# Attention scores with heads of eight: two fp32 products replaced by three bfloat16 passes over split operands

## The chip, the cores and the metric

The kernel runs on one core of one Trainium2 chip. The metric is the device time of one execution in microseconds (us). Before the change three executions took 1519.76 us in the median (1519.46 to 1520.83).

A core has five engines with their own instruction streams, each in order: TensorE (PE, matrix products; its weight loads are listed as PEld), VectorE (DVE), ScalarE (ACT), GpSimd (POOL) and SyncE (SP), which here issues most transfers (DMA). They wait for one another through semaphores. TensorE takes a stationary operand (lhsT) and streams a moving one (rhs); it writes to the eight banks of PSUM, from which DVE and ACT read. An operand that takes only 32 of the 128 partitions uses one of four row tiles of the array.

## The reference

A decoder of four layers, batch 4, sequence 256, model width 128, 16 heads of size 8, and a context of 512 rows for cross attention. Each layer is self attention, cross attention and a feed-forward part. What matters here are the attentions of layers 0 and 3, which all have this form:

```python
x = x + _L0_attn_ref(_layernorm(x), W_qkv, b_qkv, W_proj, b_proj)
x = x + _L0_xattn_ref(_layernorm(x), ctx, mask, q_w, q_b, kv_w, kv_b, proj_w, proj_b)
...
def _L0_xattn_ref(x, context, context_mask, ...):
    q = (x @ q_w + q_b).reshape(b, n, h, d)                  # h = 16, d = 8
    kv = (context @ kv_w + kv_b).reshape(b, s, 2, h, d)
    attn = jnp.einsum('bnhd,bshd->bhns', q, k) * scale
    attn = jnp.where(context_mask[:, None, None, :], -jnp.inf, attn)
    attn = jax.nn.softmax(attn, axis=-1)
    out = jnp.einsum('bhns,bshd->bnhd', attn, v).reshape(b, n, c)
    return out @ proj_w + proj_b
```

Layer 0's self attention has no mask, its cross attention a mask over keys. Layer 3's self attention makes q, k and v through a latent of width 32 and has a causal mask; its cross attention has a full mask over queries and keys. Layer 1 (with a clipped softmax), layer 2 and the feed-forward parts are not touched by the change, apart from when layer 0's expert weights are loaded.

## The kernel before

**Units.** `woven` (L394) runs a layer's attentions as a list of eight units: units 0 to 3 are the self attentions of the four batch rows (256 keys), units 4 to 7 their cross attentions (512 keys). Layers 0 and 3 use it so; layer 1 uses it for its own self attention.

**Operands.** A unit's prelude normalises x (statistics on DVE, the rest on POOL), transposes it, and makes queries (`queries`, L412: a product L343, an ACT pass L423 that scales and adds the bias, then four POOL products L426 that write `qm`, four copies of q, in each of which only one head of every group of four is not zero) and keys (`keys`, L428: a product and an ACT pass L434 into `kc`). A row tile of 32 partitions holds four heads; with the masked copy number g as one operand and all 32 partitions of `kc` as the other, a product gives the scores of one of the four.

**Rows.** `rows_of` (L454) computes scores with queries on partitions, in fp32 (L471), 512 columns in a bank of PSUM. DVE takes the maximum over keys: L478 without a mask, L482 with one (layer 3). In layer 0's cross attention the key mask is added by a bfloat16 product ahead of it (L465). `parts` (L494) splits the maxima into three bfloat16 parts on DVE, and `parts_T` (L505) transposes them on TensorE (L509) into `mT`.

**Columns.** `columns_of` (L514) computes the scores again, transposed (keys on partitions): two small bfloat16 products subtract the maxima (L530, from `mT`), one fp32 product adds the scores (L536), in layer 3 after a mask product (L523). ACT takes the exponential from PSUM (L553, or L555 with the key mask as a bias in layer 0's cross attention). `weighted` (L566; products L572) multiplies by the values and a column of ones, `divided_by_sums` (L580) transposes and divides, `added` (L604) projects and adds to x.

An fp32 product stands in the trace as two PE instructions.

**Order.** The order of TensorE's instructions is written by position. In window n, the columns of unit n run beside the rows of unit n+1 (all but the first LEAD = 2 half groups) and the first LEAD half groups of unit n+2. `beat` (L627) pairs a half group of rows (two of the four row tiles) with a half group of columns (the other two), so that all four row tiles are in use. A self window has 8 beats, the window of unit 3 has 12, cross windows 16; the last has 8 beats of columns alone. Into these the prelude of unit n+2 is spread by `front` (L677) over the first 0.95 of the window less the lead; unit 1's prelude goes into the first 0.8 of the start, where unit 0's rows run alone. Rows that have their operands not yet hold TensorE, and with it everything that is behind them. Scores use seven banks of PSUM ("s1"), a beat takes four.

**Loads around it.** `layer_0` (L2124) loads the key mask and then, in eight transfers of 1 MB, the experts' first weights `e0h` (L2129); they are used by `ffn0` (L1266), which begins by loading the second weights `e0d` (4 MB) and computes a shared expert and 32 experts. SP issues these, and the transfers of the normalised rows to DRAM (`sent`).

Of the kernel before, what the change touches and what calls it, by code (L numbers as in the profile page):

```python
# [31 lines left out]
P = 128  # L33
B, S, D, H = 4, 256, 128, 16
NT = B * S // P
SK = 512
# [33 lines left out]
def _constants():  # L70

    p = np.arange(P)
    l = np.arange(1, S + 1, dtype=np.float32)
    angle = (np.pi / 2 * l / S).astype(np.float32)
    trig = np.stack([np.sin(angle), np.cos(angle)], -1)
    trig = trig.reshape(2, P, 2).transpose(1, 0, 2).reshape(P, 4)
    ident = np.eye(P)

    tril = np.where(p[:, None] <= p[None, :], 10.0, NEG)
    m72 = np.repeat((p[:, None] // 16) == np.arange(8)[None, :], 9, axis=1)  # L80
    m4 = (p[:, None] // 32) == np.arange(4)[None, :]
    iota = np.tile(np.arange(P), (P, 1))
    gm = (p[:, None] // 8 % 4) == np.arange(4)[None, :]
    gs = -1.0 * ((p[:, None] % 4 == np.arange(4)[None, :]) & (p[:, None] % 32 < 12))
    after = p[:, None] < p[None, :]
    upto = np.concatenate([after[:, :32], p[:, None] <= p[None, :32]], 1)
    parts = (ident, tril, m72, m4, iota, trig, gm, gs, p[:, None], after, upto)
    return _cat(*[a.astype(np.float32) for a in parts])
# [3 lines left out]
    _C_IDENT, _C_TRIL, _C_M72, _C_M4, _C_IOTA, _C_TRIG, _C_GM, _C_GS, _C_PART, _C_AFTER, _C_UPTO,  # L92
    _C_END,
) = np.cumsum([0, 128, 128, 72, 4, 128, 4, 4, 4, 1, 128, 64]).tolist()


def _layout(i):
# [16 lines left out]

    w, bq = f["L0_attn_W_qkv"], f["L0_attn_b_qkv"]
    a["w0a"] = _cat(w, f["L0_attn_W_proj"], _col(bq[:128]), _col(bq[128:256]))
    w, bk = f["L0_xattn_kv_w"], f["L0_xattn_kv_b"]
    a["w0x"] = _cat(
        f["L0_xattn_q_w"], w, f["L0_xattn_proj_w"], _col(f["L0_xattn_q_b"]), _col(bk[:128])
# [12 lines left out]
        f[k + "Wq"].T, f[k + "Wk"].T, f[k + "Wv"].T, f[k + "Wo"].T,  # L132
        _col(f[k + "bq"]), _col(f[k + "bk"]),
# [8 lines left out]
    up[:32, :128] = f["L3_attn_Wq_up"].T  # L142
    up[32:64, :128] = f["L3_attn_Wk_up"].T
# [40 lines left out]
def decoder(ctx: ExitStack, tc: tile.TileContext, dr, out):  # L184
# [57 lines left out]
    partition = cst[:, _C_PART:_C_AFTER]  # L242
# [109 lines left out]
    def key_mask(pool, name, keep):  # L352

        rows_ = pool.tile([P, B * SK // 4], I32, tag="mrow", name="mrow", bufs=1)
        nc.sync.dma_start(rows_, dr[name].to_broadcast([P, B * SK // 4]))
        cols = pool.tile([P, B * NKT // 4], I32, tag="mcol", name="mcol", bufs=1)
        nc.sync.dma_start(cols, dr[name + "T"])
        out = []
        for t, dtype in ((rows_, BF16), (cols, F32)):
            t = t.bitcast(U8)  # L360
            m = pool.tile(list(t.shape), dtype, tag=f"n{t.shape[1]}", name=f"n{t.shape[1]}", bufs=1)
            if keep:
                V.tensor_scalar(m, t, 0.0, NEG, ALU.is_equal, ALU.mult)
            else:
                V.tensor_scalar(m, t, NEG, None, ALU.mult)
            out.append(m)
        return out
# [9 lines left out]
    class Unit:  # L377
# [7 lines left out]
        def __init__(u, b, nk, weights, prelude, context, q_bias=None, k_bias=None, v_bias=None,  # L385
                     rows_mask=None, row_mask=None, cols_mask=None, key_bias=None, clip=False):
            u.b, u.nk, u.weights, u.prelude, u.context = b, nk, weights, prelude, context
            u.q_bias, u.k_bias, u.v_bias = q_bias, k_bias, v_bias
            u.rows_mask, u.row_mask, u.cols_mask = rows_mask, row_mask, cols_mask
            u.key_bias, u.clip, u.nkt = key_bias, clip, nk // P  # L390
            u.mx, u.pr, u.po = None, {}, {}

            u.beside, u.after, u.within = [], [], 2.6

    def woven(pool, units, n_keys):
# [4 lines left out]
        for i in range(2):  # L400
            t = pool.tile([P, n_keys // P, H, 32], F32, tag=f"v{i}", name=f"v{i}", bufs=1)
            V.memset(t, 0.0)
            V.memset(t[:, :, :, HD : HD + 1], 1.0)
            vbuf.append(t)
            t = pool.tile([P, 2, 4, 32], BF16, tag=f"mp{i}", name=f"mp{i}", bufs=1)
            V.memset(t, 0.0)
            mbuf.append(t)

# [3 lines left out]
        def queries(u):  # L412
# [11 lines left out]
            u.qm = pool.tile([P, 4, S], F32, tag="qm", name="qm", bufs=3)  # L424
            for g in range(4):
                G.tensor_scalar(u.qm[:, g, :], q, gmask[:, g : g + 1], None, ALU.mult)  # L426

        def keys(u):  # L428
            acc = product(u.weights[1], u.key_source, "s1")
            u.kc = pool.tile([P, u.nk], F32, tag="kc", name="kc", bufs=3)  # L430
            if u.k_bias is None:
                A.copy(u.kc, acc)
            else:
                A.activation(u.kc, acc, AF.Identity, bias=u.k_bias)  # L434

# [18 lines left out]
        def rows_of(u, qt, g, half):  # L454
# [5 lines left out]
            head, tail, reads = [], [], []  # L460
            for j, r in row_tiles(half):
# [25 lines left out]
                steps = [call(score, i) for i in range(per)]  # L487
                if u.row_mask is not None:
                    steps = [mask] + steps
                head.append(steps[0])  # L490
                tail += steps[1:]
                reads.append(read)
            return [], head, tail, reads

        def parts(u):
# [3 lines left out]
            V.tensor_copy(mp[:, :, :, 0:4], u.mx)  # L499
            r1 = small.tile([P, 2, 4, 4], F32, tag="r1", name="r1")  # L500
            V.tensor_tensor(r1, u.mx, mp[:, :, :, 0:4], ALU.subtract)
            V.tensor_copy(mp[:, :, :, 4:8], r1)
            V.tensor_tensor(mp[:, :, :, 8:12], r1, mp[:, :, :, 4:8], ALU.subtract)

        def parts_T(u):  # L505
            mp = mbuf[u.n % 2]
            tp = psum[0].tile([P, 1024], BF16, tag="s1", name="s1", bufs=BANKS["s1"])
            for qt in range(2):
# [3 lines left out]
            u.mT = pool.tile([P, S], BF16, tag="mT", name="mT")  # L512
            evacuate(u.mT, tp[:, :S])

        def columns_of(u, gp, kt, half):

            first = kt * P if u.clip else 0
            masks, heads, reads = [], [[], [], []], []
            for j, r in row_tiles(half):
# [21 lines left out]
                def read(j=j, sc=sc):  # L541
# [10 lines left out]
                    elif u.key_bias is None:  # L552
# [3 lines left out]

                if u.cols_mask is not None:
                    masks.append(mask)
                if not u.clip:
                    heads[0].append(call(less, 0))  # L560
                    heads[1].append(call(less, 1))
                heads[2].append(score)
                reads.append(read)
            return masks, heads[0] + heads[1] + heads[2], [], reads
# [62 lines left out]
        def beat(*steps):  # L627

            made = [f(half) for f, half in steps]
            for k in range(3):  # L630
                for m in made:
                    for f in m[k]:
                        f()
            for pair in zip(*[m[3] for m in made]):
# [43 lines left out]
        def front(n):  # L678
# [3 lines left out]
            if n + 2 < len(units):  # L682
                out += spread(prelude(units[n + 2]), 0.0, 0.95 - lead)
# [29 lines left out]
        for n, u in enumerate(units):  # L713
            u.n = n
# [4 lines left out]
        if len(units) > 1:  # L719
            first += spread(prelude(units[1]), 0.0, 0.8)  # L720
# [545 lines left out]
    def ffn0(r, wh):  # L1266
        with ExitStack() as st:
            pool = expert_pools(st, "ffn0")
            wd = load("e0d", pool=pool)
# [854 lines left out]
    def layer_0(wh, router):  # L2124
        with ExitStack() as st:
            st.enter_context(psum_pool("ps0"))
            pool = attn_pool(st, "l0")
            neg0, neg0T = key_mask(pool, "mbk0", False)
            for i in range(0, 32, 4):  # L2129
                cols = slice(i * 512, (i + 4) * 512)  # L2130
                nc.sync.dma_start(wh[:, cols], dr["e0h"][:, cols])
# [6 lines left out]
            for u in units[:B]:  # L2138
                u.beside = [call(context_means, u.b, 0), call(context_means, u.b, 2)]
                u.beside += [call(context_scales, u.b)]  # L2140
            for u in units[B:]:
                u.beside = [call(normalise_context, u.b, i) for i in range(0, NKT, 2)]
                u.after, u.within = router.steps(pool, u.b, "s1"), 1.0
            woven(pool, units, SK)
# [17 lines left out]
    def layer_3():  # L2162
        with ExitStack() as st:
# [13 lines left out]
            woven(pool, units, SK)  # L2177
# [47 lines left out]
```

## Time and profile before

Times are of one profiled execution unless said otherwise.

| what | us |
|---|---|
| median of three executions | 1519.76 |
| the profiled execution | 1519.6 |
| its span in the trace | 1517.5 |
| layer 0, both attentions | 0 to 276 |
| layer 0, experts | 276 to 348 |
| layer 3, from the end of layer 2 | 1174 to 1517.5 |
| DVE busy in layer 0's attentions | 177.4 |
| DVE busy in layer 3 | 192.7 |
| mean granted TensorE clock | 0.927 of full speed |

The rest, from 348 to 1174 us, is layers 1 and 2. A line of the profile's groups reads: source line, engine, operation, output <- inputs with the shapes (partitions x elements; for a product partitions of contraction * partitions of output, then the moving operand), x count, then busy time in us and mean ns of one, then the idle time of the engine just before them and what ended most of it. A line of a window reads: stretch, its length, busy us and instructions of PE, PEld, DVE, ACT, POOL, granted clock, share of the DMA engines in use, GB/s. The chain of waits is the chain of work that ended last, followed back from the last instruction to what released each.

### The profile page before, as it was taken

How to read it: one execution, taken by the hardware profiler on the slowest of the kernel's cores; microseconds unless marked ns; L12 is line 12 of the kernel's file. 1: busy time of each engine (PE TensorE's matmuls, PEld its weight loads, DVE VectorE, ACT ScalarE, POOL GpSimd, SP SyncE). 2: the span in 40 equal slices, each digit the busy share in tenths (PEclk: the TensorE clock that was granted, in tenths of full speed). 3: DMA queues.
4: the chain of work that ended last, by engine and by line, in shares of the span. 5: the costliest groups of instructions: out<-in, count | busy, mean ns of one | idle time of the engine just before them, and what ended most of it. 6: DMA issues, size and time to landing. Idle time of an engine off the chain costs nothing.

```text
span 1517.5 us, 27226 instructions
## 1 busy us (share of the span) xinstructions
PE 1336.0 (88%) x10232; PEld 696.3 (46%) x10232; DVE 814.4 (54%) x2688; ACT 736.5 (49%) x1468; POOL 307.0 (20%) x433
## 2 busy tenths in 40 slices
PE   5999998796787997889999999999595699999994
PEld 3544333353353664545555565555364344433332
DVE  6687773585664447454544454460334556756633
ACT  0555666285542333267667757666021044345553
POOL 6322111354133215000000000000332513111000
PEclk7999999896996999989999999999698589999996
DMA  8000000320222124320111000000311000000000
GB/s 329 4 2 1 2 5 8 125 58 11 118 105 91 37 71 168 119 83 15 57 46 43 1 5 1 1 5 1 134 45 51 28 1 2 2 1 2 5 5 7
DMA packets 35315, 67.97 MB, mean 45 GB/s; under 512 B 5349, under 2 KB 19087, under 8 KB 33263
## 3 DMA queue, kind: packets, MB, share of 16 engines
q1 hardware_dynamic: 30770, 49.88, 9.2%
q0 software_dynamic: 3264, 6.69, 2.0%
q10 hardware_dynamic: 1152, 9.67, 1.6%
q8 instruction: 82, 1.34, 0.4%
q14 instruction: 47, 0.39, 0.1%
HBM read 49.55 MB, written 16.68 MB: 44 GB/s over the span
## 4 chain that ended last, share of the span: by engine, by line
PE 70%; DVE 10%; ACT 7%; POOL 6%; issue 4%; DMA 3%; SPq 0%; ACTq 0%; POOLq 0%; DVEq 0%
PE o L572 7%; PE s L536 7%; PE s L471 6%; PE o L1894 6%; PE g L1159 6%; PE s L1874 4%; PE f L1820 4%; PE y L1183 3%; PE s L523 3%; PE f L1806 2%; PE s L530 2%; DVE mx L478 2%; PE t L1168 2%; PE s L343 2%; PE s L1867 1%
## 5 line engine op out<-in xcount | busy, mean ns | idle before, releaser
L471 PE MATMUL s<-kc,qm 32*128 32x256 f32 (+1 forms) x1024 | 222.8, 565 | 13.6 <-DVE mx L482 6.5
L553 ACT ACTIVATE pr<-s 128x512 f32<-128x512 f32 x256 | 138.0, 596 | 187.0 <-PE s L536 184.2
L536 PE MATMUL s<-qm,kc 32*128 32x512 f32 (+1 forms) x896 | 208.8, 607 | 0.0
L293 POOL TENSOR_SCALAR ve<-mv 128x2 f32<-128x2 f32 x44 | 11.7, 266 | 789.3 <-DVE mv L288 784.3
L1831 ACT ACTIVATE ss<-ss,ntop 128x768 f32<-128x768 f32 x128 | 118.6, 928 | 90.0 <-DVE ntop L1829 89.8
L478 DVE TENSOR_REDUCE mx<-s 128x1 f32<-128x512 f32 (+1 forms) x192 | 122.6, 685 | 59.1 <-PE s L536 47.0
L572 PE MATMUL o<-pr,v 128*32 128x256 f32 (+1 forms) x1792 | 145.1, 391 | 8.9 <-ACT os L578 4.2
L471 PEld LDWEIGHTS s<-kc,qm 32*128 32x128 f32 x1024 | 91.2, 207 | 71.7 <-DVE mx L482 18.9
L1825 DVE CUSTOM_DVE_ANT_0 ss<-f,n 128x512 f32<-128x512 f32 x128 | 83.5, 689 | 68.4 <-PE f L1820 68.4
L482 DVE CUSTOM_DVE_ANT_0 junk<-s,nmif 128x512 bf16<-128x512 f32 x128 | 83.1, 688 | 47.5 <-PE s L471 47.3
L1894 PE MATMUL o<-pr,v 128*64 128x256 f32 x768 | 107.1, 392 | 1.3 <-ACT pr L1881 1.2
L555 ACT ACTIVATE pr<-s,n 128x512 f32<-128x512 f32 x128 | 80.2, 690 | 51.3 <-PE s L536 32.0
L1874 PE MATMUL s<-qT,kT 64*128 64x256 f32 x768 | 101.1, 379 | 0.0
L1881 ACT ACTIVATE pr<-s,n 128x512 f32<-128x512 f32 x128 | 80.3, 678 | 25.6 <-PE s L1874 25.3
L572 PEld LDWEIGHTS o<-pr,v 128*32 128x32 f32 x1792 | 40.1, 109 | 112.5 <-issue 83.4
L426 POOL TENSOR_SCALAR qm<-q,consts 128x256 f32<-128x256 f32 x64 | 58.5, 930 | 153.3 <-ACT q L423 123.0
L530 PE MATMUL s<-mT,selg 12*128 12x256 bf16 x768 | 80.8, 276 | 2.9 <-DVE mx L478 0.8
L1137 POOL DMA_INDIRECT xb<-sent,token x62 | 60.5, 977 | 104.1 <-PE t L1144 58.5
L1820 PE MATMUL f<-kT,qT 64*128 64x512 f32 x256 | 77.2, 625 | 2.3 <-ACT kT L273 1.1
L1813 DVE CUSTOM_DVE_ANT_0 ss<-f,nought 128x256 f32<-128x256 f32 x128 | 46.7, 421 | 55.4 <-PE f L1806 53.9
L1894 PEld LDWEIGHTS o<-pr,v 128*64 128x64 f32 x768 | 47.7, 136 | 57.2 <-issue 21.7
L536 PEld LDWEIGHTS s<-qm,kc 32*128 32x128 f32 x896 | 67.2, 194 | 6.3 <-issue 3.3
(455 smaller groups left out, 2424.9 us busy)
## 6 DMA issues: line engine op xcount, KB each, us to landing
e0h<-in_e0h SPq DMA_DIRECT2D x8, 1024.0 KB, 10.7
kd<-ahead SPq DMA_DIRECT2D x20, 256.0 KB, 2.4
vd<-ahead SPq DMA_DIRECT2D x20, 256.0 KB, 2.6
kT<-kd SPq DMA_DIRECT2D x20, 256.0 KB, 4.3
v<-vd SPq DMA_DIRECT2D x5, 1024.0 KB, 5.3
e0d<-in_e0d SPq DMA_DIRECT2D x1, 4096.0 KB
e1h<-in_e1h ACTq DMA_DIRECT2D x1, 4096.0 KB
done<-ys SPq DMA_DIRECT2D x14, 256.0 KB, 2.3
```

Of the source, the lines that this page charges most:

```text
L471: T.matmul(sc[:, i, :], lhsT=u.qm[r, g + i, qt * P : (qt + 1) * P], rhs=u.kc[r, :], start=u.row_mask is None, stop=True,)
L478: V.tensor_reduce(u.mx[:, qt, j, g : g + per], sc, AX.X, ALU.max)
L530: T.matmul(sc[:, i, :], lhsT=selg[r, gp + i, :], rhs=u.mT[r, :], start=u.cols_mask is None and i == 0, stop=False,)
L536: T.matmul(sc, lhsT=u.kc[r, kt * P : (kt + 1) * P], rhs=u.qm[r, gp : gp + 2, first:], start=u.clip, stop=True,)
L553: A.activation(dst, sc, AF.Exp)
L572: T.matmul(u.po[gp][32 * j : 32 * j + 32, i, first:], lhsT=u.v[:, kt, 4 * j + gp + i, :], rhs=u.pr[gp, kt, j][:, i, first:], start=kt + i ...
L1159: T.matmul(p[r], lhsT=xbT[b][:, r], rhs=w(512 * i), start=biases is None, stop=True,)
L1820: T.matmul(sc[h], lhsT=qT[u, c][hrow[h], qt * P : (qt + 1) * P], rhs=kT[u, c][hrow[h], :SK], start=True, stop=True,)
L1825: V.tensor_tensor_reduce(ss[qt][h][:, :SK], sc[h], neg1[:, b * SK : (b + 1) * SK], 1.0, -3e38, ALU.add, ALU.max, accum_out=mx[:, qt, h, 1:2],)
L1831: A.activation(ss[qt][h], ss[qt][h], AF.Exp, bias=ntop[:, qt, h, c : c + 1], accum_out=total[:, qt, h, c : c + 1],)
L1874: T.matmul(sc[h][:, i, :], lhsT=kT[u, c][hrow[h], kt * P : (kt + 1) * P], rhs=qT[u, c][hrow[h], :], start=False, stop=i == 1,)
L1894: T.matmul(po[u, g][hrow[h], i, :], lhsT=v[u][:, kt, n * hd : (n + 1) * hd], rhs=pr[u, g, kt, h][:, i, :], start=kt + i == 0, stop=kt + i ...
```

## The change

In layers 0 and 3, for all units but the first of each layer:

- q and k are each written as a sum of three bfloat16 parts (`in_parts`, on POOL: copy, subtract, copy, subtract).
- The parts go to DRAM (one transfer for q, one for k) and are read back so that, in a row tile of 32 partitions, partition 4·d + i holds element d of a head in slot i: the q operand `q3[c]` repeats part c in the slots 0 to 2, the k operand `kk` holds the parts 0 to 2 in them; the four heads of the row tile lie side by side in the free dimension. One product of 32 partitions thus makes three of the nine products of parts, and three of them, one for each `q3[c]`, make all nine. That takes nine reads for q and three for k.
- Slot 3 carries constants (`rest`, loaded once) on one side and, on the other, the key mask (layer 0's cross attention, one read more) or the parts of the maxima. These are brought by eight transposes and one DVE addition (`qmax`), so that the subtraction of the maximum and the key mask need no products of their own. The exponential has no bias any more.
- The weights' columns are permuted in the inputs (`byd`), so that a head's eight elements lie where the reads want them.
- `beat` deals out the products round by round, rows and columns in turn.
- The prelude of a split unit is spread over the first 0.4 of a self window or 0.55 of a cross window, unit 1's over the first 0.3 of the start.
- Three sets of parts are kept. In layer 0 they lie in the second half of the tile of `e0h`, and so does the key mask: the first half of `e0h` is loaded beside unit 0, the second half in `ffn0`, between the two halves of `e0d`. In layer 3 they lie in the normalised context and `w2kv`, which are no longer used.

```diff
+        def in_parts(src, tag, m):
+            n = src.shape[1]
+            t = pool.tile([P, 3, m], BF16, tag=tag, name=tag)[:, :, :n]
+            G.tensor_copy(t[:, 0], src)
+            G.tensor_tensor(src, src, t[:, 0], ALU.subtract)
+            G.tensor_copy(t[:, 1], src)
+            G.tensor_tensor(t[:, 2], src, t[:, 1], ALU.subtract)
+            return t
...
         def queries(u):
...
-            u.qm = pool.tile([P, 4, S], F32, tag="qm", name="qm", bufs=3)
+            if u.split:
+                u.q3 = qbuf[u.n % 3]
+                to = qd[u.n % 3]
+                nc.sync.dma_start(to.rearrange("c f n -> f c n"), in_parts(q, "qp", S))
+                for c in range(3):
+                    for i in range(3):
+                        nc.sync.dma_start(
+                            u.q3[c][i::4], to[c].rearrange("(x g) n -> x g n", g=4)
+                        )
+                return
+            u.qm = pool.tile([P, 4, S], F32, tag="qm", name="qm", bufs=1 if split else 3)
...
         def keys(u):
...
+            if u.split:
+                u.kk = kbuf[u.n % 3]
+                to = kd[u.n % 3][:, :, : u.nk]
+                nc.sync.dma_start(to.rearrange("c f n -> f c n"), in_parts(u.kc, "kp", SK))
+                for c in range(3):
+                    nc.sync.dma_start(
+                        u.kk[c::4, :, : u.nk], to[c].rearrange("(x g) n -> x g n", g=4)
+                    )
+                if u.row_mask is not None:
+                    nc.sync.dma_start(
+                        u.kk[15::32, :, : u.nk],
+                        u.row_mask[0:4].unsqueeze(1).to_broadcast([4, 4, u.nk]),
+                    )
...
         def rows_of(u, qt, g, half):
...
+                def part(n, r=r, sc=sc):
+                    i, c = n // 3, n % 3
+                    T.matmul(
+                        sc[:, i, :], lhsT=u.q3[c][r, g + i, qt * P : (qt + 1) * P],
+                        rhs=u.kk[r, g + i, : u.nk], start=n == 0, stop=n == 3 * per - 1,
+                    )
+
+                if u.split:
+                    for n in range(3 * per):
+                        rounds.setdefault(2 * n // per, []).append(call(part, n))
...
         def parts_T(u):
...
+            if u.split:
+                for qt in range(2):
+                    for g in range(4):
+                        T.transpose(
+                            tp[:, g * S + qt * P : g * S + (qt + 1) * P],
+                            mp[:, qt, g].rearrange("p j c -> p (j c)"), identb,
+                        )
+
+                u.qmax = pool.tile([P, 4, S], BF16, tag="qmax", name="qmax")
+                V.tensor_tensor(
+                    u.qmax, tp.rearrange("p (g n) -> p g n", g=4), u.q3[2], ALU.add
+                )
+                return
...
         def columns_of(u, gp, kt, half):
...
+                def part(n, r=r, sc=sc):
+                    c, i = n // 2, n % 2
+                    T.matmul(
+                        sc[:, i, :], lhsT=u.kk[r, gp + i, kt * P : (kt + 1) * P],
+                        rhs=(u.q3[0], u.q3[1], u.qmax)[c][r, gp + i, :],
+                        start=u.cols_mask is None and n == 0, stop=n == 5,
+                    )
...
+                if u.split:
+                    for n in range(6):
+                        rounds.setdefault(n, []).append(call(part, n))
...
         def front(n):
...
-                out += spread(prelude(units[n + 2]), 0.0, 0.95 - lead)
+                u = units[n + 2]
+                end = 0.95 - lead if not u.split else 0.4 if units[n].nk < SK else 0.55
+                out += spread(prelude(u), 0.0, end)
...
-            u.n = n
+            u.n, u.split = n, split and n > 0
...
-            first += spread(prelude(units[1]), 0.0, 0.8)
+            first += spread(prelude(units[1]), 0.0, 0.3 if split else 0.8)
...
     def ffn0(r, wh):
...
-            wd = load("e0d", pool=pool)
+            wd = pool.tile([P, 32 * 256], F32, tag="e0d", name="e0d", bufs=1)
+            for i in range(0, 32, 16):
+                cols = slice(i * 256, (i + 16) * 256)
+                nc.sync.dma_start(wd[:, cols], dr["e0d"][:, cols])
+                if i == 0:
+                    cols = slice(16 * 512, 32 * 512)
+                    nc.sync.dma_start(wh[:, cols], dr["e0h"][:, cols])
...
     def layer_0(wh, router):
...
-            for i in range(0, 32, 4):
-                cols = slice(i * 512, (i + 4) * 512)
-                nc.sync.dma_start(wh[:, cols], dr["e0h"][:, cols])
+            lent = Lent(wh[:, 16 * 512 :])
+            neg0, neg0T = key_mask(pool, "mbk0", False, lent)
+
+            def loads():
+                for i in range(0, 16, 4):
+                    cols = slice(i * 512, (i + 4) * 512)
+                    nc.sync.dma_start(wh[:, cols], dr["e0h"][:, cols])
...
+            units[0].beside += [loads]
...
-            woven(pool, units, SK)
+            woven(pool, units, SK, True, lent)
```

## The prediction

> **What bounds the kernel now.** I read the totals and the chain of waits first, then the costliest groups, then busy time by unit window (a window runs from one transpose of the maxima, L509, to the next: layer 0 at 34, 54, 74, 95, 126, 163, 201 and 240 us; layer 3 at 1211, 1235, 1260, 1284, 1317, 1357, 1403 and 1454), then the timeline of one beat and the chain inside one window.
>
> ```profile
> PE 1336.0 (88%) x10232; PEld 696.3 (46%) x10232; DVE 814.4 (54%) x2688; ACT 736.5 (49%) x1468; POOL 307.0 (20%) x433
> PE 70%; DVE 10%; ACT 7%; POOL 6%; issue 4%; DMA 3%; SPq 0%; ACTq 0%; POOLq 0%; DVEq 0%
> L471 PE MATMUL s<-kc,qm 32*128 32x256 f32 (+1 forms) x1024 | 222.8, 565 | 13.6 <-DVE mx L482 6.5
> L536 PE MATMUL s<-qm,kc 32*128 32x512 f32 (+1 forms) x896 | 208.8, 607 | 0.0
> L478 DVE TENSOR_REDUCE mx<-s 128x1 f32<-128x512 f32 (+1 forms) x192 | 122.6, 685 | 59.1 <-PE s L536 47.0
> L553 ACT ACTIVATE pr<-s 128x512 f32<-128x512 f32 x256 | 138.0, 596 | 187.0 <-PE s L536 184.2
> L426 POOL TENSOR_SCALAR qm<-q,consts 128x256 f32<-128x256 f32 x64 | 58.5, 930 | 153.3 <-ACT q L423 123.0
> ```
>
> TensorE carries 70% of the chain; the exponentials and maxima mostly wait for it ("<-PE"). The next view gives PE, PEld, DVE, ACT and POOL busy in three windows and in layer 3's start, then clock, DMA share, GB/s.
>
> ```profile
> 54.00:74.00 20.00, 18.88 (x221) 10.12 (x221) 15.26 (x44) 11.24 (x23) 6.84 (x10) 1.00 0.01 2
> 163.00:201.00 38.00, 37.47 (x393) 14.86 (x394) 27.35 (x69) 23.70 (x42) 7.33 (x10) 1.00 0.02 5
> 1174.00:1211.00 37.00, 21.38 (x102) 11.98 (x103) 18.62 (x93) 2.14 (x6) 22.65 (x26) 0.50 0.10 29
> 1357.00:1403.40 46.40, 45.24 (x392) 16.70 (x390) 30.69 (x105) 24.07 (x42) 6.14 (x8) 1.00 0.01 1
> ```
>
> Inside windows PE is over 94% busy; DVE and ACT have a third spare in cross windows. Now one beat of layer 0's cross attention (start, length, PE instructions):
>
> ```profile
> 189.41 0.39 PE L465 MATMUL s<-n,onesb 1*128 1x512 bf16 x2
> 189.41 0.39 PE L530 MATMUL s<-mT,selg 12*128 12x256 bf16 x4
> 189.63 0.59 PE L471 MATMUL s<-kc,qm 32*128 32x512 f32 x2
> 189.64 0.59 PE L536 MATMUL s<-qm,kc 32*128 32x512 f32 x2
> 190.06 0.59 PE L471 MATMUL s<-kc,qm 32*128 32x512 f32 x2
> 190.07 0.59 PE L536 MATMUL s<-qm,kc 32*128 32x512 f32 x2
> 190.59 0.66 PE L587 MATMUL s<-consts,os 128*128 128x128 f32 x4
> ```
>
> Four row tiles start together, two of rows and two of columns. An fp32 product is two instructions, 0.43 us apart. The score part is 0.22 + 2×0.43 + about 0.1 = 1.19 us of a beat of 1.92 to 3.2.
>
> Last, the chain inside the window at 64 us:
>
> ```profile
> 65.87 0.49 ACT q L423
> 66.36 0.08 issue
> 66.44 2.73 POOL qm L426 x3
> 69.18 0.05 issue
> ```
>
> So making the next unit's operands (q product, ACT, POOL) is already near the path in self-attention windows.
>
> **What the Trainium skill says.** "TensorE: Matmul & The Clock Gate", Part 3 (packing small matmuls): row tiles at partitions 32i run concurrently, some 4 ns apart. The trace agrees: the four start within 10 ns. "TensorEngine Tiling (Array Packing)", PSUM Bottleneck: tiling doesn't speed the reading of PSUM, which may become the limit. The reads here, 0.685 (DVE) and 0.596 (ACT) per bank, are the next limit. The first page's Part 1 (the clock gate): after some 3.4 us of idleness the array runs at half clock. Layer 3's start shows it: 0.50. "DMA: Bandwidth & Descriptors", Anatomy of one DMA: waits happen on the issuing sequencer, so a read that must see a write holds SP. No row of before isolates that.
>
> **The change part by part.**
>
> *Score products.* Rows: three bf16 passes for two fp32 ones (in layer 0's cross units the mask product goes too). Columns: six 256-column bf16 products for two of the mask kind and one fp32. Prices: bf16 256 columns 0.12 us start to start (L530, raw rows at 189.413 and 189.532), bf16 512 about 0.21 (the mask product L523, two in 0.60). Three 512s are 0.64, six 256s 0.72; they lie beside each other in different row tiles, so with the same 0.1 the part is about 0.8: −0.4 per beat. Bounds: −0.25 if the seven score banks set the pace (a beat takes four, and its last waits for the first DVE or ACT read), −0.5 if the bf16 weight loads hide wholly. I take −0.4. DVE (1.3 to 1.6 per beat) and ACT (1.2) then stand just under the beat. Windows that keep the gain: in each layer 12 beats of unit 3, 16 each of units 4, 5, 6, 8 of unit 7: 68, two layers 136. 136×0.4 = **−54**.
>
> *Operands.* Four POOL products (L426, 0.91 each) go; eight POOL copies and subtractions, a DRAM write and nine reads for q, a write and three reads for k come, all on SP in this order: q write, nine q reads (the first waits for the write), k write, k reads. The first rows of the unit after next wait for all of it. Chain from the q product: 1.6 to q (64.82 to 66.35 before), POOL 3.0 (two copies at 0.47 by the copy L1123, two subtractions about 0.9 by L426, one estimate each), q write 2.1 (64 KB takes 1.5, 256 KB 2.4 in the DMA view; this is 196), nine reads at 0.37 issue = 3.4 (SP's issues before follow at 0.32 to 0.48), k write 2.3, k issues 1.1, landing 1.8: **15.2 us**, bounds 14 and 19.
>
> *Where that is late.* A self window has 8 beats. The q product stands after the second, the waiting rows in the seventh, and TensorE is in order: everything queued behind them waits too, the window's own columns, weighted products and maxima transposes. Only 4 beats cover the chain. Window after = chain + 4 shortened beats + about 1.2 for the clock falling in the stall. Layer 0: 15.2 + 4×2.1 + 1.2 = 24.8 against 19.6, 19.9, 20.7 (the third needs 512 keys, +0.8): +15. Layer 3: 15.2 + 4×2.7 + 1.2 = 27.2 against 24.6, 25.0, 23.5: +8.7. Sum **+24**. So units 0 to 2 give back more than their products gain, which I therefore left out of the 136 beats.
>
> *Starts.* Unit 0's columns stand behind unit 1's first rows. In layer 0 unit 1's q came at 26.2 us, k at 31.0; the new chain is ready near 42 instead of 33, with a cold unit 0 in front: **+7.5** (0 to 12). Layer 3's start is paced by POOL and DVE (POOL 22.65 busy of 37): **+2** (0 to 6).
>
> *Cross windows.* The q product stands after six beats, the rows after fourteen: 8×2 = 16 us against 15 to 16. **+2** for units 4 and 5 together (0 to 6).
>
> *At nothing.* POOL's change per unit (four products at 0.91 out, eight passes near 0.7 in, +2) counts only through the chain above (7 of 38 us busy in a cross window). Max subtraction: eight transposes and one DVE addition over 1024 columns instead of two and one copy; the mask kinds on DVE strided; +0.7 DVE per unit, one beat ahead of its use. If not covered, 14 units × 0.7 = 10. Exp without a bias: 596 for 690, ACT isn't last. Twelve constant loads at the start, behind the key mask: hidden by unit 0 (SP had no other work; bound +3, within the start's range). Half of e0h (4 of 8 MB) loads in the next stage because the parts lie in its place: 4 MB at some 10 to 12 us (8 MB took to 40 us at the start) from the last score near 267, needed at 295; if late, +5. The other half follows in window 0, ahead of unit 3's write by about 12 us: hidden, just.
>
> *Sum.* −54 + 24 + 9.5 + 2 = −18.5. Span 1517.5 − 18.5 = 1499, plus the 2.1 that the profiled run (1519.6) has around it: **1501**. The run's 1519.6 is 0.2 under the median, 1519.76, so no correction.
>
> **The rivals.**
> (B) *Reading sets the pace.* DVE and ACT take over and a beat gains 0.25: −34 + 24 + 9.5 + 2 = about 0: **1520**. For: bank cycle, 1.55 us by the two reads of 0.685 and 0.6 with hand-over. Against: ACT's and DVE's large idle beside PE.
> (C) *The operands are never late*: SP issues fast, landings overlap, no stall: −54 + 3 for starts: **1468**. For: DMA share is 0.01 to 0.02 in these windows. Against: the serial order on SP, and 4 beats of cover.
> (A) *Slower: the operand chain.* Place: the SP queue between q product and rows. If each issue costs 0.48 and a write of small pieces takes 4.3 (the kT reads from DRAM did), the chain is about 19. About 12 places (six self windows, two starts, four cross windows) each lengthen by the excess: 3.8×12 = 46 over the main case: **1547**. It decides from 16.7 us on (18.5/12 = 1.5 above 15.2). For: 13 DMAs in one queue, two DRAM round trips in series. Against: small transfers landed in 1.5 to 2.4.
> (D) That the new products don't run as three parallel passes (a fp32 path left, a row tile blocked): 1530; the order of instructions shows them, so within A's share.
>
> **How the numbers follow.** Main 0.50 (1501; own range 1485 to 1517), C 0.15, B 0.12, A with D 0.23. A measurement can tell about 0.2%, 3 us, from no change. Faster: 0.48 of main + 0.15 + 0.03 of B = 0.66. Same: B's 0.05 and 0.01 of main = 0.06. Slower: 0.04 of B, 0.23 + 0.01 = 0.28. Range: from C's 1468 to 1540, which leaves out half of A (0.11) and the faster part of C (0.07).
>
> **What would show it.** Cross beats near 0.4 us shorter (162 to 201 in about 31 us); self windows of 25 to 27 us with PE waiting for DMA in the seventh beat and a clock below 1.00 there; unit 0's window beginning near 42; e0h's second half landed before its first expert. Cross windows also waiting for DMA would make (A) right; no DMA waits at all (C); waits of PE for DVE and ACT reads with an unchanged beat (B).

## The result, and the profile after

The changed kernel took 1535.51 us in the median of four executions (1533.45 to 1539.08), the kernel before 1519.61 beside it (four, 1517.89 to 1520.83): ratio 1.0108, 95% interval 1.0083 to 1.0133. The forecast was 1501, faster. The time lies in the stated range, on the other side of no change: it went the way of rival (A).

The span of the profiled execution grew from 1517.5 to 1535.4 us. First the page's totals, the chain by engine and the group of the row products:

```profile
PE 1283.8 (84%) x11340; PEld 708.6 (46%) x11340; DVE 826.5 (54%) x2697; ACT 721.7 (47%) x1461; POOL 325.8 (21%) x489
PE 62%; DVE 12%; POOL 7%; ACT 6%; issue 5%; DMA 5%; SPq 2%; ACTq 0%; POOLq 0%; DVEq 0%
L579 PE MATMUL s<-e0h 32*128 32x512 bf16 (+1 forms) x672 | 80.6, 370 | 41.7 <-DMA e0h<-kp 37.1
```

TensorE has 52 us less to do and the kernel is 18 us longer: its share of the chain fell from 70% to 62%, and DMA and SP rose from 3% to 7%. The row products (L579 now) stand 37.1 us behind "e0h<-kp", the read that lays the k parts into the borrowed tile. Before there was no such releaser.

Next, the four windows of the changed kernel that answer to the four shown of before (same columns): unit 1's in layer 0, unit 5's in layer 0, layer 3's start, and unit 5's in layer 3:

```profile
75.01:102.65 27.64, 19.17 (x302) 10.61 (x301) 15.78 (x43) 10.63 (x21) 8.83 (x16) 0.81 0.49 186
193.44:230.75 37.31, 32.32 (x466) 17.20 (x463) 27.71 (x68) 20.75 (x40) 9.29 (x14) 0.91 0.16 48
1197.20:1228.59 31.39, 17.62 (x107) 10.59 (x107) 17.09 (x89) 1.67 (x5) 20.20 (x27) 0.50 0.21 57
1382.36:1427.60 45.24, 39.01 (x492) 17.99 (x493) 31.50 (x104) 23.83 (x42) 8.14 (x12) 0.96 0.13 36
```

The self window is 8 us longer, with PE idle for 8.5 of 27.6 us, and the granted clock is 0.81 instead of 1.00. In layer 0's cross window PE is idle for 5 us, in layer 3's for 6.

Window by window, from one transpose of the maxima to the next (layer 0's start from 0, layer 3's from its first product; the last window to the end of layer 0's attention and to layer 3's last score product):

| us | start | u0 | u1 | u2 | u3 | u4 | u5 | u6 | u7 |
|---|---|---|---|---|---|---|---|---|---|
| layer 0 before | 34.3 | 19.6 | 19.9 | 20.7 | 31.5 | 37.1 | 37.8 | 39.1 | 33.7 |
| layer 0 after | 46.6 | 28.5 | 27.6 | 27.1 | 28.9 | 34.8 | 37.3 | 34.1 | 27.3 |
| layer 3 before | 33.7 | 24.6 | 25.0 | 23.5 | 32.9 | 40.3 | 46.4 | 50.4 | 35.1 |
| layer 3 after | 31.4 | 29.9 | 29.1 | 28.9 | 30.3 | 35.6 | 45.2 | 47.7 | 32.6 |

The windows of units 0 to 2 (self windows) lost 37.6 us (22.9 in layer 0, 14.7 in layer 3), the starts 10.0, the windows of units 3 to 7 gained 30.2 (16.8 and 13.5); with 1.6 more between the two layers and 1.1 less in the tail that is the span's 17.9.

The products themselves did what they should. One beat of layer 0's cross attention, from the timeline (start, length, instructions):

```profile
213.30 0.39 PE L579 MATMUL s<-e0h 32*128 32x512 bf16 x2
213.31 0.39 PE L681 MATMUL s<-e0h 32*128 32x256 bf16 x4
213.53 0.38 PE L579 MATMUL s<-e0h 32*128 32x512 bf16 x2
213.54 0.38 PE L681 MATMUL s<-e0h 32*128 32x256 bf16 x4
213.74 0.38 PE L579 MATMUL s<-e0h 32*128 32x512 bf16 x2
213.75 0.38 PE L681 MATMUL s<-qmax,e0h 32*128 32x256 bf16 x4
214.06 0.42 PE L708 MATMUL o<-pr,v 128*32 128x256 f32 x4
```

Three rounds 0.22 us apart, and the weighted products follow 0.76 us after the first. In the beat shown of before what follows the score products begins 1.18 us after the first.

What fills the self window is SP. Its queue in the window from 75 us (start, time in issues, line):

```profile
86.59 0.38 SPq L494 DMA_DIRECT2D qp<-qp  x1
89.77 5.56 SPq L497 DMA_DIRECT2D e0h<-qp  x9
95.42 0.53 SPq L515 DMA_DIRECT2D kp<-kp  x1
97.64 1.83 SPq L517 DMA_DIRECT2D e0h<-kp  x3
```

The q product began at 82.61, the waiting rows at 101.25: 18.6 us. Nine reads take 5.56 us to issue, not 3.4, and the k write, whose parts POOL had finished at 88.87, stands behind them until 95.42. (The other five self windows take 17.9 to 18.7 us for the same chain.) TensorE's waits in the same window say the same from the other end (in all, times, longest):

```profile
PE s L579 <- DMA e0h<-kp: 7.3, 1, 7.3
```

### The profile page after: what moved, and what is told of

It is laid out like the page before. It is cut to its first block, busy times and chain, and to the rows that moved or that the text cites. A ratio compares the mean times of both kernels' runs of the same rounds, so it can differ in the third digit from the quotient of the medians.

```text
span 1535.4 us, 29900 instructions
## 1 busy us (share of the span) xinstructions
PE 1283.8 (84%) x11340; PEld 708.6 (46%) x11340; DVE 826.5 (54%) x2697; ACT 721.7 (47%) x1461; POOL 325.8 (21%) x489
## 4 chain that ended last, share of the span: by engine, by line
PE 62%; DVE 12%; POOL 7%; ACT 6%; issue 5%; DMA 5%; SPq 2%; ACTq 0%; POOLq 0%; DVEq 0%
PE o L708 6%; PE o L2041 6%; PE g L1300 6%; PE s L579 5%; PE s L2021 5%; PE f L1967 4%; PE s L681 3%; PE y L1324 3%; PE s L645 2%; PE f L1953 2%; POOL xn L318 2%; PE s L360 2%; DVE mx L568 2%; POOL back L1373 2%; PE t L1309 2%
## 5 line engine op out<-in xcount | busy, mean ns | idle before, releaser
L675 ACT ACTIVATE pr<-s 128x512 f32<-128x512 f32 x384 | 206.4, 597 | 272.5 <-PE s L681 196.7
L310 POOL TENSOR_SCALAR ve<-mv 128x2 f32<-128x2 f32 x44 | 11.7, 267 | 776.7 <-DVE mv L305 771.2
L708 PE MATMUL o<-pr,v 128*32 128x256 f32 (+1 forms) x1792 | 149.1, 404 | 7.4 <-ACT os L714 6.2
L579 PE MATMUL s<-e0h 32*128 32x512 bf16 (+1 forms) x672 | 80.6, 370 | 41.7 <-DMA e0h<-kp 37.1
L572 DVE CUSTOM_DVE_ANT_0 junk<-s,nmif 128x512 bf16<-128x512 f32 x128 | 82.9, 687 | 37.8 <-PE s L681 30.1
L2028 ACT ACTIVATE pr<-s,n 128x512 f32<-128x512 f32 x128 | 80.3, 679 | 24.5 <-PE s L2021 24.3
L2041 PEld LDWEIGHTS o<-pr,v 128*64 128x64 f32 x768 | 48.0, 136 | 56.6 <-issue 20.3
L2021 PEld LDWEIGHTS s<-qT,kT 64*128 64x128 f32 x768 | 67.8, 189 | 5.8
L572 DVE CUSTOM_DVE_ANT_0 junk<-s,nmcau 128x256 bf16<-128x256 f32 x128 | 46.4, 421 | 37.8 <-PE s L658 16.9
L579 PEld LDWEIGHTS <-e0h 32*128 32x128 bf16 x672 | 28.0, 100 | 76.0 <-issue 72.5
L681 PE MATMUL s<-e0h 32*128 32x256 bf16 x704 | 58.6, 283 | 4.8 <-DVE mx L568 4.6
L328 PE MATMUL s<-consts,xn 128*128 128x128 f32 x64 | 19.5, 361 | 47.2 <-POOL xn L318 47.2
L318 POOL TENSOR_SCALAR xn<-x,mv,rs 128x128 f32<-128x128 f32 x72 | 57.6, 807 | 3.8
```

The source lines that it names most:

```text
L318: (on or V).tensor_scalar(d, s, mv[:, i, 0:1], rs[:, i : i + 1], ALU.subtract, ALU.mult)
L572: V.tensor_tensor_reduce(junk[:, : u.nk], sc[:, i, :], u.rows_mask(qt), 1.0, -3e38, ALU.add, ALU.max, accum_out=u.mx[:, qt, j, g + i : g + ...
L579: T.matmul(sc[:, i, :], lhsT=u.q3[c][r, g + i, qt * P : (qt + 1) * P], rhs=u.kk[r, g + i, : u.nk], start=n == 0, stop=n == 3 * per - 1,)
L675: A.activation(dst, sc, AF.Exp)
L681: T.matmul(sc[:, i, :], lhsT=u.kk[r, gp + i, kt * P : (kt + 1) * P], rhs=(u.q3[0], u.q3[1], u.qmax)[c][r, gp + i, :], start=u.cols_mask is ...
L708: T.matmul(u.po[gp][32 * j : 32 * j + 32, i, first:], lhsT=u.v[:, kt, 4 * j + gp + i, :], rhs=u.pr[gp, kt, j][:, i, first:], start=kt + i ...
```

## The experiments

Ratios are to the kernel before, timed on the same chip in the same batch, since its own median went from 1517.8 to 1527.3 between chips. The changed kernel has 1.0108.

| run | ratio, 95% interval |
|---|---|
| reads left out | 0.9715 (0.9686 to 0.9743) |
| both writes first | 1.0020 (1.0005 to 1.0034) |
| q reads on ACT | 1.0308 (1.0263 to 1.0353) |
| only cross units split | 1.0179 (1.0147 to 1.0211) |
| three q reads | 0.9870 (0.9845 to 0.9894) |
| three q reads, writes first | 0.9810 (0.9788 to 0.9832) |
| three q reads, earlier prelude | 0.9814 (0.9781 to 0.9847) |
| feed-forward steps spread | 1.0081 (1.0053 to 1.0108) |
| all three | 0.9778 (0.9747 to 0.9809) |
| all three, steps last | 0.9779 (0.9746 to 0.9812) |
| early in self windows alone | 0.9760 (0.9730 to 0.9790) |
| and a shorter start | 0.9729 (0.9706 to 0.9751) |

Theory 1 was that TensorE waits for operands behind SP's queue, theory 2 that reading PSUM by DVE and ACT had become the bound.

**The reads left out.** All reads in `queries` and `keys` go (those of k and of the key mask aren't shown here); the constant loads fill the whole operand buffers with zeros.

```diff
-                for c in range(3):
-                    for i in range(3):
-                        nc.sync.dma_start(
-                            u.q3[c][i::4], to[c].rearrange("(x g) n -> x g n", g=4)
-                        )
...
-                    dr["rest"][m : m + 32, :n],
+                    dr["rest"][32:33, :n].to_broadcast([P, n]),
```

> The reads that lay the parts out are left out (q, k and the key mask; the operand buffers are filled with zeros once at the start), so all scores of the split units are zero; parts, writes, products, maxima and exponentials run as before. Theory 1 (the operand chain on SP makes TensorE wait; the products themselves gain): with nothing to wait for, the six self windows fall below those of before the change and cross beats lose 0.3 to 0.4 us each, 1450 to 1475 us. Theory 2 (reading PSUM by DVE and ACT has become the bound, and takes back the products' gain): no less than 1500 us, with the cross windows of layer 0 as long as in the changed kernel (29, 35, 37, 34 us).

1485.31 us. Between the two, nearer to theory 1: the part from layer 0's end to layer 3's start is 10.8 us longer than in the changed kernel here (the tokens go to other experts when all scores are zero), so layers 0 and 3 alone lose more than the ratio says. Layer 0's windows of units 3 to 7 became 28.0, 31.8, 31.3, 32.2 and 27.3 us: 28.7 less than before the change, which is the 0.4 us per beat of the prediction (68 × 0.4 = 27.2). Layer 3's were 29.4, 35.6, 45.0, 47.6 and 32.6: within 1 us of those of the changed kernel. So layer 0 waited for operands, and layer 3's cross windows for something else. The self windows did not all fall below those of before: layer 3's did (22.1, 21.6 and 20.7 us), layer 0's were 23.0, 18.5 and 21.6, in sum 63.1 against 60.3 before and 83.2 in the changed kernel. Of the 22.9 us that they had lost, 20.1 came back with the reads gone.

**Both writes first.** `queries` only writes; `keys` writes, then issues all reads.

```diff
-                for c in range(3):
-                    for i in range(3):
-                        nc.sync.dma_start(u.q3[c][i::4], ...)
                 return
...
                 nc.sync.dma_start(to.rearrange("c f n -> f c n"), in_parts(u.kc, "kp", SK))
+                for c in range(3):
+                    for i in range(3):
+                        nc.sync.dma_start(u.q3[c][i::4], ...)
```

> Both writes of a unit's parts stand before its twelve reads, so SP doesn't wait for the k write to land between them. Theory 1: the q reads start some 1.2 us later (they now wait for the k parts too), the 2.7 us of the k write leave the chain: about 1.5 us less in each of some 10 places that wait for operands, 1515 to 1525 us. Theory 2: no change, 1533 to 1538 us.

As theory 1: 1529.92, that is 0.9% less than the changed kernel by the ratios; layer 0's self windows fell to 26.1, 25.4 and 26.2 us.

**The q reads on ACT.** One word: `nc.scalar.dma_start` for the nine.

> The nine q reads are issued by ACT instead of SP. Theory 1: q and k come in parallel, 3.5 us less per place, 25 to 35 us less, but ACT stands 5.6 us per unit in issues, and waits for the q write, with exponentials behind it: 1505 to 1530 us. Theory 2: slower than the changed kernel, since ACT is loaded further, 1540 us or more.

1574.56, a miss. ACT's waits in the whole kernel hold this row (its layer 0 reads, as far as an exponential follows), and its timeline the next:

```profile
ACT pr L675 <- DMA e0h<-qp: 36.9, 4, 10.2
```

```profile
112.25 5.85 ACTq L497 DMA_DIRECT2D e0h<-qp  x9
```

The waits count all the time between ACT's last pass and its next one, the issues included: in this place its pass ends at 109.67, it waits 2.6 us for the q write, and then issues for 5.85. In the other windows, the starts apart, the wait is 0 to 4.6 us and the issues 5.6 to 6.9, up to 10.2 together, with exponentials behind them. Unit 4's window in layer 0 grew to 44.4 us. I had priced the issues, named the wait without a price, and not asked what exponentials that come some 8 us late cost TensorE. The layer 0 start did fall (46.6 to 40.5 us), where ACT had nothing else to do.

**Only the cross units split.**

```diff
-            u.n, u.split = n, split and n > 0
+            u.n, u.split = n, split and n >= B
```

The three fp32 q operands of the self units lie in the borrowed tile too (layer 0), since the pool has no room for them; 2.5 instead of 4 MB of e0h load beside unit 0.

> Only units 4 to 7 are split; self attention keeps its fp32 products and its operands. Theory 1: the starts (12 us in layer 0) and the first two self windows of each layer (9, 8, 5, 4 us) are as before the change, the third still waits for unit 4's parts, cross windows keep their gain: 1495 to 1503 us. Theory 2: the self windows lose time through reading too, which goes in the same way; but their idle PE time is not waiting for DMA, and cross windows of layer 0 stay at 35 to 37 us.

1557.8, half a hit. Where only self units are at work the windows are back: layer 0's start 36.7, units 0 and 1 20.6 and 19.9 us; layer 3's 24.0 and 25.0. But layer 0's third and fourth windows took 49.8 and 48.0 us. TensorE's waits in the third, from 77 to 127 us:

```profile
PE s L575 <- DMA e0h<-qp: 11.1, 1, 11.1
PE s L575 <- DMA e0h<-kp: 10.0, 1, 10.0
```

L575 is the fp32 row product of unit 3, which waits here for the reads of unit 4's parts into other columns of the same tile. I take that to come from my placing both in it; another place wasn't tried, so the cause isn't shown, and this run doesn't say what splitting cross units alone is worth.

**Three q reads.** The three operands of a unit side by side, one read per slot instead of three.

```diff
+                for i in range(3):
+                    nc.sync.dma_start(
+                        qall[u.n % 3][i::4].rearrange("x (c m) -> x c m", c=3),
+                        qd[u.n % 3].rearrange("c (x g) n -> x c (g n)", g=4),
+                    )
```

> The nine q reads of a unit are merged into three, each with the same bytes in total (32 partitions of three pieces of 2 KB): the three q operands lie side by side, so one read fills one slot of all three. If each issue costs SP its 0.64 us whatever it moves, six issues less shorten the operand chain by 3.7 us; with some 10 places that wait for it the kernel takes 25 to 37 us less than the changed kernel, and falls 10 to 20 us below the kernel before. If the issue's cost goes with the pieces, nothing changes (1.1% above the kernel before). If reading PSUM is what holds the self windows, nothing changes either.

1504.05: 2.4% or 36 us less than the changed kernel, as for a cost per issue. SP's queue in this run shows the same bytes in a third of the time:

```profile
84.06 1.89 SPq L502 DMA_DIRECT2D e0h<-qp  x3
86.00 0.59 SPq L521 DMA_DIRECT2D kp<-kp  x1
88.92 1.82 SPq L523 DMA_DIRECT2D e0h<-kp  x3
```

The windows of units 4 to 6 in layer 0 reached those without reads (31.8, 31.3, 32.2), here with operands that are not zero. This alone turns the change from a loss into a gain.

**Three q reads with the writes first**, and **with an earlier prelude.** The second edit:

```diff
-                end = 0.95 - lead if not u.split else 0.4 if units[n].nk < SK else 0.55
+                end = 0.95 - lead if not u.split else 0.2 if units[n].nk < SK else 0.3
```

> As the run with three q reads, and both writes stand before the reads. The writes' order gave about 13 us by itself beside the kernel before; with the reads merged the k write's landing is a larger part of what is left, so 8 to 15 us less than with three reads alone, 1.5% to 2% below the kernel before. If the two shorten the same wait and cover has been reached in most places, less than 5 us.

> As the run with three q reads, and the prelude of a split unit is spread over the first 0.2 of a self window and 0.3 of a cross window instead of 0.4 and 0.55, so q's product stands one beat earlier in self windows, and three in cross windows. If the self windows still wait for operands after the merge, some 2 us less in each of six, and the last DMA waits of layer 0's cross windows go: 10 to 18 us less than with three reads. If the merge already covers them, no change; if the early prelude makes DVE and POOL late with what it needs itself, slower.

1495.36 and 1492.26, both as expected. Self windows were 22.8, 21.6, 22.3 and 25.1, 23.4, 25.4 in the first; 21.5, 20.3, 25.3 and 23.4, 22.2, 21.0 in the second.

**Feed-forward steps of layer 3 spread** (`quantised_steps(pool, u.b), 0.8` to 1.6 on the changed kernel).

> As the changed kernel, and only the feed-forward steps of layer 3 are spread over 1.6 windows instead of 0.8, so that DVE's quantising stands further behind the POOL and ACT work that it reads. If DVE standing in its order before them is what takes back the gain in layer 3's cross windows (maxima queue behind, TensorE waits 3.5 us at a time), the windows of units 5 and 6 lose 2 to 5 us each, 4 to 10 us in all. If reading by DVE as such is the bound there, no change.

Inconclusive: 1536.35, not to be told from the changed kernel. Unit 5's window fell from 45.2 to 42.8 us, unit 6's stayed (47.5).

**All three**, and **all three with layer 3's steps last**: the second hangs the steps of all four batch rows on the last unit.

```diff
             for u in units[B:]:
-                u.after, u.within = quantised_steps(pool, u.b), 0.8
+                last.after = last.after + quantised_steps(pool, u.b)
+            last.within = 3.2
```

> Three q reads, both writes ahead of them, and the earlier prelude together. Beside the kernel before, three reads gave 19 us, the writes' order some 9 more, the earlier prelude some 12 more. If they shorten the same waits, which by now are mostly covered, the sum stays within 5 us of the better of the two pairs: 1485 to 1495 us, 2 to 2.5% below the kernel before. If each still removes its own wait, 1478 to 1484. It can't go below the run without reads by much (42 us below the kernel before).

> As the run with all three, and the feed-forward steps of layer 3's four batch rows all stand behind the last unit, instead of beside the windows of units 5, 6 and 7. They are the same work, so the end grows by what they took beside other work. If DVE, waiting in its order for POOL and ACT in these steps, holds the maxima and takes back the gain there, the windows of units 5 and 6 fall from 46 and 48 us to 36 to 41. If the plain reading of PSUM by DVE is the bound, they fall by no more than the steps' own DVE time, some 5 us in unit 5's, and the beats stay at their length.

1487.19, as expected if the three shorten the same waits, and 1490.21. Between the two, layer 3's windows of units 5, 6 and 7 fell from 48.8, 47.8 and 32.6 us to 42.8, 36.8 and 25.3, and what follows the last score product grew from 27.2 to 51.1. So the move saves nothing in sum (24.3 us less, 23.9 more); what it shows is what fills these windows. Unit 6's, with all three, has this wait of PE and these of DVE:

```profile
PE s L585 <- DVE mx L578: 5.0, 3, 3.5
```

```profile
DVE am L2161 <- ACT h L2194: 2.9, 1, 2.9
DVE am L2161 <- POOL xq L318: 2.8, 1, 2.8
```

and in the two runs this busy time (all three first, then steps last):

```profile
1377.80:1425.70 47.90, 42.47 (x523) 19.35 (x520) 31.09 (x105) 23.78 (x42) 2.52 (x4) 0.93 0.02 4
```

```profile
1364.50:1401.30 36.80, 36.51 (x495) 16.40 (x496) 25.30 (x84) 18.09 (x35) 2.53 (x4) 1.00 0.01 2
```

Of 11.1 us, 6.0 are busy time of TensorE (28 instructions moved away, and the granted clock is 1.00 instead of 0.93); the other 5.1 are the wait of TensorE for maxima, which is gone with the steps. DVE takes its instructions in order: while the quantising (L2161) waits for POOL or ACT, maxima that are ready to be read stand behind it. With DVE busy for 25.3 us of 36.8 and TensorE for 36.5, reading as such isn't the bound. In unit 5's window one such step stayed (its POOL wait of 3.7 us and a PE wait of 4.0 are still there), hence 42.8.

**Early in self windows alone** (0.2 and 0.55, steps over 1.2), and **with a shorter start**: only unit 1's four constant loads ahead of its parts on SP, and unit 1's parts made on DVE.

```diff
+        if split:
+            constants(1)
...
+                nc.sync.dma_start(..., in_parts(q, "qp", S, V if u.n == 1 else G))
...
+                if u.n < 3:
+                    constants((u.n + 1) % 3)
```

> As the run with all three, with the prelude in cross windows at 0.55 again and layer 3's feed-forward steps over 1.2 windows instead of 0.8. In the run with the earlier prelude alone unit 5's window in layer 3 was 1.3 us longer and layer 0's cross windows 1 us longer than with three reads, since the prelude met other work; with the reads merged the cross windows need no earlier operands. 3 to 6 us less than the run with all three if that is so, the same if not.

> As the run with the prelude early in self windows alone, and of the start two things change: only unit 1's four constant loads stand ahead of its parts on SP (the other eight follow later units' reads), and unit 1's parts are made on DVE instead of POOL. In the changed kernel the twelve loads end at 33.5 us, the moment at which the POOL parts are done too, so each alone hides the other. If the two are what is left of the start's loss, layer 0's start falls from 42.7 to 37 to 40 us, and the kernel takes 3 to 5 us less than that run. If unit 0's rows or the two DRAM trips set the start, less than 1 us.

1487.07: not to be told from all three (a miss; unit 5's window fell to 41.5 us and unit 6's rose to 51.4). And 1477.42 against 1517.8 before: the lowest ratio of all, 2.7% below the kernel before, with an interval that overlaps that of the run ahead of it. Layer 0's start fell from 42.7 to 39.8 and layer 3's from 32.5 to 27.2 us. The second I had not expected. The two edits were not tried apart, and for layer 0's start it stays open which of them did it. For layer 3's the traces point to POOL: in the run ahead of this one the constant loads had been issued by 1155 us and the q write came at 1182, so they held nothing up. But POOL issued the last four of eight gathers of routed rows only after it had made the parts; DVE stood 9.2 us in its order for such rows, and TensorE up to 6.4 us at a time for the maxima behind them. With the parts on DVE all eight gathers follow one another, and these waits are 3.0 and 1.8 us.

## Why the prediction was wrong

From the −18.5 predicted to the +17.9 of the span are 36.4 us: 21.8 of them in the windows of units 3 to 7 (−52 with the "+2" for cross windows, −30.2 measured), 13.6 in the self windows (+24, +37.6), and 1.0 in the starts and the rest. Two steps failed: the price of the operand chain, and DVE's cost taken as its busy time alone.

**The score products: right in the beat, wrong in the sum.** In beats without a wait the score part went from 1.19 us (1.35 is about as frequent) to 0.76 (predicted 0.8), in layer 3 from 1.73 to 1.30 (most frequent values, from the first score product to the next instruction of another kind). The term "136 × 0.4 = −54" came out as −30.2. In layer 0 it was −16.8, and −28.7 with the reads out: operands were late there. In layer 3 it was −13.5, and hardly more, −14.8, with the reads out. TensorE's busy time in layer 3's five windows did fall, from 198.2 to 173.3 us, but its idle time grew from 6.8 to 18.2, and most of that is waits for maxima (in all, times, longest; the first two lines are before, the third after):

```profile
PE s L471 <- DVE mx L482: 1.6, 2, 1.1
PE s L523 <- DVE mx L482: 0.7, 1, 0.7
PE s L579 <- DVE mx L572: 11.7, 8, 3.5
```

DVE's order behind the feed-forward steps took this back: 11.2 of the 11.7 us stand in the windows of units 5 and 6, beside such steps, and the run with the steps last shows for unit 6's that the waits go with the steps. I had looked at DVE's busy share, found it just under the beat, and not asked what DVE waits for in its order. Rival (B) had the engine but not the mechanism: where no step stands in the way, TensorE is busy throughout (36.5 of 36.8 us).

**The operand chain: the price that failed.** "Nine reads at 0.37 issue = 3.4" measured 5.6 in the self window shown and 6.35 in layer 0's unit 5's. The chain of 15.2 us was 18.6 in the self window at 75 us: 4.0 to the parts (predicted 4.6), 3.2 for the q write (2.1), 5.6 for the reads, 2.2 for the k write, 3.6 for its reads and landing (2.9). The q write took 2.0 to 2.2 us in the other five self windows, where the chain is 17.9 to 18.7 us, in the mean of all six 18.3. The 3.2 fall together with the first half of `e0h`: SP issues it at 72.8 us, behind unit 2's reads, and the DMA engines are 0.49 busy in this window (0.15 to 0.21 in the other five). So "hidden, just" was probably short by 1 us; no run tries it apart. In unit 5's window of layer 0 the chain was 20.7 from the product at 208.62 to the rows at 229.35. All lie beyond the 16.7 us at which rival (A) decides. I had carried a price over from SP's other issues, whose shape is another, and named 0.48 only as a case against me.

**Where it is late: right.** Only four beats cover it, the seventh beat waits for DMA, and the clock falls (0.81). With 18.3 for 15.2, the prediction's own formula gives 27.9 us for layer 0's windows, 28.7 for the third, and 30.3 for layer 3's; measured were 28.5, 27.6, 27.1 and 29.9, 29.1, 28.9. So 37.6 us were lost instead of 24. (As listed, the terms of the chain add up to 15.3, and layer 3's windows to +8.5, not +8.7; neither matters here.)

**Starts.** +12.3 in layer 0 (7.5, bounds 0 to 12) and −2.3 in layer 3 (+2, bounds 0 to 6). "Hidden by unit 0" was wrong for the constant loads: the twelve ended at 33.4 us, between unit 1's q parts (32.5) and its k parts (33.7). The last run shows some 3 us for that and for POOL together.

**Cross windows.** "+2 for units 4 and 5" was 9 us in layer 0, by the windows with and without reads (34.8 and 37.3 against 31.8 and 31.3), and nothing in layer 3, whose longer beats cover the chain.

**At nothing.** The second half of `e0h` and what else changed between the layers' attentions cost at most the 1.6 us there, which can't be told from no change: that stretch varies from 900.8 to 906.5 us among the profiles of the runs from three q reads on.

**The rival that came true** was (A), by its place and its tipping point; its 1547 was 12 us too high. With the measured 18.3 its formula gives 1538, but that this is near is partly luck: (A) counted excess chain in layer 3's start and cross windows, and the first got shorter while the second lost to DVE's order. Runs took the cause away one piece at a time: six issues less gave 36 us; beside that, either the k write out of the series or an earlier product gave a further 0.6%, both together 0.9%; and with no reads at all layer 0's windows of units 3 to 7 showed the whole predicted gain.

## What to carry to other kernels

A cheaper operand format must be charged for making its operands: write the chain from the product to the first use in order, with each DMA issue as an instruction of its queue, and count the work that covers it. Merge transfers before moving them to another engine: a queue that has to wait for a write holds everything behind the wait, and an engine with other work pays for the wait and for the issues. When TensorE's work shrinks, look at the in-order neighbours for instructions that wait on a third engine; busy shares don't show them. Moving the waiting instructions elsewhere shortened the windows here, but not the kernel.

## What the runs showed that I had not expected

A read of 32 partitions cost SP about 0.62 us in its queue whether it carried one piece of 2 KB per partition (nine in 5.56 us) or three (three in 1.89). The eight loads of x, 128 partitions each, had taken 0.47 (3.74 us). And moving unit 1's eight elementwise instructions from POOL to DVE shortened layer 3's start by 5.4 us, though DVE has more to do there (18.9 us instead of 17.1): DVE no longer stands as long for rows that POOL gathers late.
